# A fused transformer block on one core: zero matmuls in TensorE's waits, and a new order of the setup

## The chip, the cores and the metric

The kernel runs on one core of a Trainium2 chip. Its engines work side by side, each through its own list of instructions in order: TensorE (PE, matmuls; its weight loads are shown as PEld), VectorE (DVE), ScalarE (ACT), GpSimd (POOL) and SyncE (SP), which here only issues DMAs. Engines wait for one another by semaphores. The metric is device microseconds for one execution; several executions are run and their median is compared.

## The reference

One block of a diffusion transformer, for 16 samples (B) of 256 tokens (N) and width 256 (H), with 16 heads of 16, all in float32:

```
c_proj = silu(c) @ W_mod + b_mod                 # six vectors a sample
shift_a, scale_a, gate_a, shift_m, scale_m, gate_m = split(c_proj, 6)

x_norm = ln(x) * (1 + scale_a) + shift_a
q, k, v = split(x_norm @ W_qkv + b_qkv, 3)
x = x + gate_a * (softmax(q k^T / 4) v @ W_proj + b_proj)

q_c = ln(x) @ W_qc + b_qc
k_c, v_c = split(ln(context) @ W_kvc + b_kvc, 2)
x = x + softmax(q_c k_c^T / 4) v_c @ W_cproj + b_cproj

h = gelu((ln(x) * (1 + scale_m) + shift_m) @ W_mlp1 + b_mlp1)
out = x + gate_m * (h @ W_mlp2 + b_mlp2)
```

## The kernel before

**Units.** An attention of one sample is a unit: a self-attention ("s") or a cross-attention ("c"). There are 32, in the order s0, s1, s2, s3, then s4, c0, s5, c1 and so on; the last four are c12 to c15. After them comes the MLP of all samples in chunks.

**Precision.** Matmuls that must be exact run as three products of split operands (a high and a low part in float32r): `mm3` and `mm3_tok` issue six matmuls for one half of a projection. The high parts are made on ACT, the low parts on DVE or POOL. Matmuls of plain float32 (the zeros, the small columns of the setup, ps_ga, ps_pb) are written as two records each in the trace.

**A unit's work.** `layernorm` has three steps: statistics (DVE), reciprocal root (a power on POOL) and application. `transposed` turns the result on PE (tile psT), and makes its high part (xTh, ACT) and low part (xTl, DVE). `to_stack` projects to K or Q, makes h_k or h_q on ACT and l_k or l_q on DVE, and `send` copies their rows by DMA into a stack (tile big; three stacks are used in turn). A stack is zeroed once at the start, and row 63 of each half holds ones in K and the negative maxima in Q. `to_v` projects V into tile v, whose other columns are ones. Then come eight beats in which `s_tile` computes scores for the row maxima (tile s, PE) and one DVE reduction (tile mx) takes them; `m_part` transposes the maxima (psm), and two DMAs put them into the stack. In the eight beats after that, `t_part` computes the transposed scores (tile st, PE), ACT takes the exponential (tile pt), and `av_part` multiplies by V (tile o). Normalisation and projection out follow.

**The order of the work.** `beat(n, k)` writes beat k of unit n: the exponentials of unit n beside the maxima of unit n + 1, and pieces of the projections of units n + 2 and n + 3. There, projections run in lanes (`lane`, `lanes`): a lane contracts over half of the array's rows, and two lanes run side by side. `n` begins at -1, where only the maxima of unit 0 are made. All engines keep the written order.

**What stands ahead of the beats.** A string of words, `PRE`, gives the order of the setup; `SL` adds words to single beats. Here `L0a`, `L0b`, `L0d` are the layernorm steps of unit 0 (d: applied on DVE), `T0t`, `T0h`, `T0l` its transposes, high and low part, `K0a`, `K0b`, `K0l` the two halves of its projection K and the low part, `K0x0`, `K0y1p` and so on the sends of a half of the rows (with p: issued by POOL, else by SP), `z1kp` the zeroing of K's half of stack 1 on POOL, `ld2` the load of x of unit 2, `one0` the rows of ones of stack 0.

**The setup.** `setup_first` is a generator: each word `first` runs it to its next `yield`. It loads two parts of W_mod and three of W_qkv, then x of unit 1, takes silu of the condition, and has `busy(7)` and `busy(1)`, matmuls of zeros (wz, tile ps_warm). `cols_wide` makes scale and shift as rows (16 x 256), copies them on ACT and transposes them back to columns; `cols` makes the bias columns bk, bq, bv. `setup_rest` is a generator too: it loads all the remaining weights of the attention (wga, wp_f, wkc_f, wqc_f, wvc_f, wcp_f) and biases in its first step, then makes the gate (ps_ga, ps_pb, tile gb, stored to gd), and splits the weights one after another.

The projections of unit 0, and K of unit 1, stand ahead of the beats; Q and V of unit 1 and K of unit 2 run in lanes inside the eight beats n = -1. Issues of one engine are in order, so what stands behind a waiting instruction waits too; a DMA that SP issues waits on SP for its data.

Of the kernel before, what the change touches and what calls it, by code (L numbers as in the profile page):

```python
# [21 lines left out]
def pixart_block(  # L22
# [32 lines left out]
    E_ = {'M': ((-17, -12, -10, -1, 1), (0, 3, 4, 7, 9), (8, 11, 13, 15)), 'CUT': 8, 'LN': {'s': 'pool', 'c': 'pool', 'q': 'pool'}, 'ON': (1, 1, 1), 'L0': -16, 'L1': 1, 'S0': -7, 'A0': 0, 'T0': 1, 'H': (7, 11, 14, 15), 'S1': 5, 'A1': 7, 'L2': 9, 'T1': 9, 'S2': 32, 'AP': 23, 'DV': (0, 1), 'HP': (0, 0), 'BZ': {}, 'AV': {1: [(1, 2), (1, 3)], 9: [(0, 0), (0, 1)]}, 'AHEAD': (0, 0, 0, 0, 0, 2), 'W1P': [(-9, 1), (-8, 1), (-7, 1), (-6, 1), (-5, 1), (-5, 5), (-4, 1), (-4, 3), (-4, 5), (-3, 1), (-3, 3), (-3, 5), (-2, 1)], 'W2P': [(-4, 7), (-3, 0), (-3, 4), (-3, 6), (-3, 7), (-2, 2), (-2, 4), (-2, 6), (-1, 0), (-1, 1)], 'XP': 1, 'IL': 1, 'MF': 0, 'SH': 4, 'RAMP': 1, 'HA': 1, 'MP': 16, 'W': (7, 1, 0, 0), 'PRE': 'z0q first L0a L0b L0d z1kp z0k ld2 L1a first first T0t ld3 L1b z1qp first T0h T0l first one0 K0a z2kp z2qp rest K0b K0x0 L1d K0y0p first K0l K0l0 Q0a Q0b T1a Q0l Q0x0 Q0l0 Q0y0p Q0y1p T1b K0l1 Q0l1 K0y1p V0a K0x1p V0b K1a K1b Q0x1 ld4', 'SL': {(-1, 0): 'one1 one2', (-1, 2): 'first', (-1, 4): 'rest', (-1, 6): 'rest', (0, 0): 'rest', (0, 2): 'rest', (0, 4): 'rest', (0, 6): 'rest', (1, 3): 'rest'}}  # L55
# [49 lines left out]
    load_x(0)  # L105
    brow = const.tile([32, P], F32, name="brow")
    SP.dma_start(brow, bias_rows)
# [26 lines left out]

    def cols(dst, src, rhs, bias, name):

        pst = ps_gen(f"ps_{name}")
        n = 0
        for w in src:
            for t in range(w.shape[2] // P):  # L140
                for k in range(KC):
                    PE.matmul(pst[:, n * B:(n + 1) * B], w[:, k, t * P:(t + 1) * P], rhs[:, k],
                              start=(k == 0), stop=(k == KC - 1))
                n += 1
        DVE.tensor_tensor(dst, pst[:, :n * B].rearrange("p (n b) -> p n b", b=B),
                          bias.unsqueeze(2).to_broadcast([P, n, B]), ALU.add)
# [15 lines left out]
    def busy(n):  # L162
        if n == 0:
            return
        pst = ps_gen("ps_warm")
        for _ in range(n):
            PE.matmul(pst[:, :P], wz, wz, start=True, stop=True)

    def setup_first():

        ts = [work.tile([P, 2, KC, H], F32, tag="pt", name=f"wf{i}", bufs=5) for i in range(3)]
        wm = {c: stage(W_mod, c * H, "", t=ts[0][:, c]) for c in (1, 0)}
        wk, wq = [stage(W_qkv, c, "", t=ts[1][:, i]) for i, c in enumerate((H, 0))]
        load_x(1)
        wv = stage(W_qkv, 2 * H, "", t=ts[2][:, 0])
        dummy = const.tile([P, 2], F32, name="dummy")
        ACT.activation(dummy, mhalf, AF.Tanh)
        ACT.activation(th, c_sb, AF.Tanh, scale=0.5)
        DVE.scalar_tensor_tensor(th, th, 1.0, c_sb, ALU.add, ALU.mult)
        DVE.tensor_scalar(th, th, 0.5, None, ALU.mult)  # L180
        for v in vts:
            POOL.memset(v[:, :, :, HD:], 1.0)
        yield
        busy(E_['W'][0])
        pst = ps_gen("ps_silu")
        for k in range(KC):
            PE.transpose(pst[:, k * B:(k + 1) * B], th[:, k * P:(k + 1) * P], ident[:B, :B])
        ACT.copy(sT.rearrange("p k b -> p (k b)"), pst[:, :KC * B])
        pst = ps_gen("ps_brow")
        PE.transpose(pst[:, :32], brow, ident[:32, :32])  # L190
        ACT.copy(bT, pst[:, :32])
        busy(E_['W'][1])
        ACT.copy(Wk[0], wk)
        POOL.tensor_tensor(Wk[1], wk, Wk[0], ALU.subtract)
        scale = cols_wide(cpT[:, 2:4], wm[1], sT, bT[:, BMOD + 2:BMOD + 4], "scale")
        shift = cols_wide(cpT[:, 0:2], wm[0], sT, bT[:, BMOD:BMOD + 2], "shift")
        next(scale)
        ACT.copy(Wq[0], wq)
        POOL.tensor_tensor(Wq[1], wq, Wq[0], ALU.subtract)
        next(shift)  # L200
        busy(E_['W'][2])
        yield
        next(scale, None)
        DVE.tensor_scalar(sc1[:, 0], cpT[:, 2:4], 1.0, None, ALU.add)
        yield
        next(shift, None)
        busy(E_['W'][3])
        yield
        cols(bqkv[:, 2:4], [wk], cpT, bT[:, BQKV + 2:BQKV + 4], "bk")
        yield  # L210
        cols(bqkv[:, 0:2], [wq], cpT, bT[:, BQKV:BQKV + 2], "bq")
        ACT.copy(Wv[0], wv)
        DVE.tensor_tensor(Wv[1], wv, Wv[0], ALU.subtract)
        yield
        cols(bqkv[:, 4:6], [wv], cpT, bT[:, BQKV + 4:BQKV + 6], "bv")

    def setup_rest():
        gb = work.tile([B, 2, 2, H], F32, tag="pt", name="gb", bufs=5)
        gA, bb = gb[:, 0], gb[:, 1]
        bc = const.tile([1, H], F32, name="bc")  # L220
        wg, wp = stage(W_mod, 2 * H, "wga", "g", 3), stage(W_proj, 0, "wp_f", "g", 3)
        wkc, wqc = stage(W_kvc, 0, "wkc_f", "g", 3), stage(W_qc, 0, "wqc_f", "c", 2)
        wvc, wcp = stage(W_kvc, H, "wvc_f", "x1", 5), stage(W_cproj, 0, "wcp_f", "x1", 5)
        SP.dma_start(bb[:, 0], b_mod[2 * H:3 * H].partition_broadcast(B))
        SP.dma_start(bb[:, 1], b_proj.partition_broadcast(B))
        SP.dma_start(bc, b_cproj.partition_broadcast(1))
        yield
        pst = ps_gen("ps_ga")
        for k in range(KC):
            PE.matmul(pst[:B, :H], sT[:, k], wg[:, k], start=(k == 0), stop=(k == KC - 1))  # L230
        DVE.tensor_tensor(gA[:, 0], pst[:B, :H], bb[:, 0], ALU.add)
        yield
        pst = ps_gen("ps_pb")
        for k in range(KC):
            PE.matmul(pst[:B, :H], bqkv[:, 4 + k], wp[:, k], start=(k == 0), stop=(k == KC - 1))
        DVE.tensor_tensor(gA[:, 1], pst[:B, :H], bb[:, 1], ALU.add)
        DVE.tensor_tensor(gA[:, 1], gA[:, 1], gA[:, 0], ALU.mult)
        SP.dma_start(gd[:, 0:2], gA)
        yield
        split(Wp[0], Wp[1], wp)  # L240
        yield
        split(Wkc[0], Wkc[1], wkc)
        yield
        split(Wqc[0], Wqc[1], wqc)
        yield
        split(Wvc[0], Wvc[1], wvc)
        yield
        pst = ps_gen("ps_cb")
        for k in range(KC):
            PE.matmul(pst[:1, :H], bT[:, BKVC + 2 + k:BKVC + 3 + k], wcp[:, k],  # L250
                      start=(k == 0), stop=(k == KC - 1))
        DVE.tensor_tensor(bc, pst[:1, :H], bc, ALU.add)
        SP.dma_start(cd, bc)
        split(Wcp[0], Wcp[1], wcp)
# [139 lines left out]
    def to_stack(W, src, bias, dst, which, name):  # L394
# [8 lines left out]
        def first():  # L403
            o.ps = ps_gen(f"ps_{name}")
            mm3(o.ps[:, 0:N], W, 0, src.xT)

        def second():
            mm3(o.ps[:, N:], W, 1, src.xT)
            high()
# [30 lines left out]
        o.parts = [first, second, low]  # L440
        o.low_pool = low_pool
# [6 lines left out]
    def to_v(W, src, vt, name):  # L448
# [3 lines left out]
        def first():  # L452
            o.ps = ps_gen(f"psv_{name}")
# [122 lines left out]
    sp = psum.tile([P, 2, 512], F32, tag="s", name="s", bufs=1)  # L576
# [36 lines left out]

    st = psum.tile([P, 2, 512], F32, tag="st", name="st", bufs=1)
# [227 lines left out]
    w1, w2, first, rest = mlp_w1(), mlp_w2(), setup_first(), setup_rest()  # L842
# [8 lines left out]
    for n, v in (("0", u0), ("1", u1), ("2", u2)):  # L851
# [6 lines left out]
        word["L" + n + "d"] = lambda v=v: v.ln[0].steps[2]("dve")  # L858
        word["T" + n + "a"] = lambda v=v: (v.T[0].turn(), v.T[0].high())
        word["T" + n + "b"] = v.T[0].low  # L860
    for n, v in (("0", u0), ("1", u1), ("2", u2)):
        word["T" + n + "t"], word["T" + n + "h"], word["T" + n + "l"] = v.T[0].parts
        word["T" + n + "p"] = v.T[0].low_pool
        for c in "KQ":
            o = getattr(v, c)
            word[c + n + "l"] = o.parts[2]
            word[c + n + "p"] = o.low_pool
# [16 lines left out]
    for n in range(9):  # L884
        word[f"b{n}"] = lambda n=n: busy(n)
    for n in (2, 3, 4):
        word[f"ld{n}"] = lambda n=n: load(units[n])
    word["rest"] = lambda: next(rest, None)
    word["first"] = lambda: next(first, None)
# [32 lines left out]
    def beat(n, k):  # L922
        cur, prev, nxt = unit(n), unit(n - 1), unit(n + 1)
# [8 lines left out]
        soon = q3 if n < 0 else None  # L932
        q3T = q3 if not soon else None
# [5 lines left out]
        if k == 0 and q2:  # L939
            if n >= 0:  # L940
                q2.K.high()
# [27 lines left out]
        elif k == 1:  # L969
# [5 lines left out]
            if soon:  # L975
                soon.ln[0].steps[0]()
        elif k == 2:
# [8 lines left out]
            if soon:  # L986
                soon.ln[0].steps[1]()
                soon.ln[0].steps[2]()
# [9 lines left out]
        elif k == 4:  # L998
# [9 lines left out]
            if soon:  # L1008
                soon.T[0].turn()
                soon.T[0].high()  # L1010
                soon.T[0].low()
# [146 lines left out]
```

## Time and profile before

| | us |
|---|---|
| median of three runs | 828.48 (826.91 to 828.72) |
| the profiled execution, its time | 827.59 |
| its span, first to last instruction | 825.8 |
| PE busy | 782.7 |
| first matmul of s that waits (unit 0) | 28.57 |
| first matmul of s of unit 1, start of beat (0, 0) | 49.61 |
| first exponential (unit 0) | 50.90 |
| first exponential of unit 1 / of unit 2 | 68.87 / 87.96 |

A row of the timeline has the start and the duration in us, the engine, the line (L51 for all, the helper that records operations), the operation, the tile written and the tiles read, their shapes and the number of instructions merged; in brackets stands how long the engine had been idle before and what ended that. A row of the windows has the stretch, its length, the busy time and number of instructions of PE, PEld, DVE, ACT and POOL, the granted clock of TensorE (1.00 is full), the busy share of the DMA engines, and GB/s. A busy PE is not PE at its peak: at half the granted clock the same matmuls show as longer.

### The profile page before, as it was taken

What the parts mean: (1) busy time and instruction counts of PE and PEld (TensorE: products, weight loads), DVE (VectorE), ACT (ScalarE), POOL (GpSimd) and SP (SyncE); (2) the same over time, 40 slices, a digit from 0 to 9 for tenths busy, and PEclk for the clock granted to TensorE, in tenths of its full rate; (3) what the DMA queues carried; (4) which work ended last, traced back from release to release, by engine and by line L of the source; (5) the groups of instructions that cost most, each with busy time, mean ns of one, the idle gap of its engine ahead of it and who ended that gap; (6) DMA issues with size and microseconds to landing.
All of it is one profiled execution on the core that took longest, in us unless ns stands there. A gap on an engine that the chain in (4) does not pass through costs nothing.

```text
span 825.8 us, 23598 instructions
## 1 busy us (share of the span) xinstructions
PE 782.7 (95%) x9395; PEld 657.3 (80%) x9395; DVE 605.9 (73%) x1058; ACT 585.5 (71%) x1024; POOL 458.2 (55%) x398
## 2 busy tenths in 40 slices
PE   7789999999999999999999999999889999999997
PEld 6667777787787877777777787877558999999997
DVE  8488788888878788888788888777664566666562
ACT  3146888787887878888787888887556666666663
POOL 7125565663646546475563668655445666566663
PEclk9699999999999999999999999999899999999999
DMA  6434444343444535345344554434311222212211
GB/s 212 112 93 118 118 116 136 88 129 103 133 122 112 149 93 146 104 121 153 88 136 113 153 142 126 143 110 118 105 54 40 67 62 78 64 53 77 77 35 56
DMA packets 89841, 87.87 MB, mean 106 GB/s; under 512 B 9506, under 2 KB 85444, under 8 KB 89732
## 3 DMA queue, kind: packets, MB, share of 16 engines
q1 hardware_dynamic: 89492, 85.71, 36.9%
q8 instruction: 74, 1.21, 0.7%
q0 software_dynamic: 240, 0.66, 0.3%
q14 instruction: 35, 0.29, 0.1%
HBM read 26.97 MB, written 8.46 MB: 43 GB/s over the span
## 4 chain that ended last, share of the span: by engine, by line
PE 69%; DVE 19%; issue 5%; POOL 3%; DMA 2%; ACT 1%; SPq 0%; POOLq 0%; ACTq 0%
PE s L51 15%; PE o L51 12%; DVE mx L51 12%; PE ph L51 10%; PE st L51 9%; PE ps_q L51 4%; PE ps_kc L51 3%; PE ps_k L51 3%; PE ps_P_s L51 2%; PE ps_qc L51 2%; PE ps_v_s L51 2%; DVE xTl_s L51 1%; PE ps_P_c L51 1%; PE psm L51 1%; PE psT_m L51 1%
## 5 line engine op out<-in xcount | busy, mean ns | idle before, releaser
L51 DVE TENSOR_REDUCE mx<-s 128x4 f32<-128x1024 f32 x256 | 313.1, 1223 | 115.7 <-PE s L51 110.6
L51 ACT ACTIVATE pt<-st 128x1024 f32<-128x1024 f32 x256 | 260.9, 1019 | 47.2 <-PE st L51 40.3
L51 PE MATMUL s<-big 63*128 63x256 f32 x1024 | 125.1, 314 | 23.4 <-DVE mx L51 16.3
L51 PEld LDWEIGHTS s<-big 63*128 63x128 f32 x1024 | 82.9, 189 | 61.5 <-DVE mx L51 35.7
L51 PE MATMUL o<-pt,v 128*32 128x256 f32 x2048 | 125.5, 386 | 2.9 <-DVE A_s L51 2.9
L51 POOL TENSOR_TENSOR hl<-hf,hh 128x512 fp32r<-128x512 f32 x64 | 89.0, 1399 | 55.5 <-ACT hh L51 54.5
L51 PE MATMUL st<-big 64*128 64x256 f32 x1024 | 108.1, 283 | 2.0 <-ACT pt L51 2.0
L51 PEld LDWEIGHTS o<-pt,v 128*32 128x32 f32 x2048 | 60.8, 110 | 45.3 <-DVE A_s L51 5.2
L51 PEld LDWEIGHTS st<-big 64*128 64x128 f32 x1024 | 82.9, 189 | 3.8 <-ACT pt L51 2.9
L51 ACT COPY oT<-o 128x512 f32<-128x512 f32 x63 | 36.9, 586 | 47.6 <-PE o L51 47.6
L51 ACT ACTIVATE hf<-ph,bT 128x256 f32<-128x256 f32 x120 | 50.3, 473 | 28.1 <-PE ph L51 28.1
L51 ACT ACTIVATE hh<-ph,bT 128x256 fp32r<-128x256 f32 x120 | 50.4, 471 | 24.8 <-PE s L51 13.0
L51 POOL TENSOR_TENSOR xTl_as<-y_as,xTh_as 128x512 fp32r<-128x512 f32 x16 | 20.3, 1270 | 64.1 <-ACT y_as L51 64.1
L51 POOL TENSOR_TENSOR xTl_c<-y_c,xTh_c 128x512 fp32r<-128x512 f32 x16 | 20.6, 1290 | 62.0 <-PE s L51 52.9
L51 PE MATMUL ph<-wqch,wself 128*128 128x256 f32 x256 | 51.8, 285 | 0.0
L51 PE MATMUL ph<-wkch,wself 128*128 128x256 f32 x256 | 51.8, 286 | 0.0
L51 POOL TENSOR_TENSOR xTl_ac<-y_ac,xTh_ac 128x512 fp32r<-128x512 f32 x16 | 20.5, 1281 | 54.8 <-ACT y_ac L51 50.9
L51 PE MATMUL s<-big,hh 128*128 128x256 f32 x256 | 47.4, 282 | 0.0
L51 PE MATMUL st<-big,hh 128*128 128x256 f32 x256 | 47.2, 281 | 0.0
L51 DVE TENSOR_SCALAR xn_m<-x,mv_m,rs_m 128x256 f32<-128x256 f32 x32 | 38.2, 1234 | 10.8 <-POOL rs_m L51 10.8
L51 PEld LDWEIGHTS ph<-wqch,wself 128*128 128x128 f32 x256 | 42.0, 191 | 0.4 <-issue 0.4
L51 PEld LDWEIGHTS ph<-wkch,wself 128*128 128x128 f32 x256 | 41.9, 191 | 0.4
(234 smaller groups left out, 2373.3 us busy)
## 6 DMA issues: line engine op xcount, KB each, us to landing
big<-h_kc SPq DMA_DIRECT2D x64, 128.0 KB
big<-h_qc SPq DMA_DIRECT2D x64, 128.0 KB
big<-h_q SPq DMA_DIRECT2D x62, 128.0 KB
big<-h_k SPq DMA_DIRECT2D x61, 128.0 KB
x<-in_x_dram SPq DMA_DIRECT2D x16, 256.0 KB
big<-l_k SPq DMA_DIRECT2D x32, 128.0 KB
big<-l_q SPq DMA_DIRECT2D x32, 128.0 KB
c<-in_ctx_dram SPq DMA_DIRECT2D x16, 256.0 KB
```

Source lines behind the costliest of these rows:

```text
L51: i = f(*a, **k)
```

## The change

Three things are edited.

**Setup.** The generator `setup_first` becomes single words (`load`, `silu`, `turn`, `brow`, `scale`, `sc1`, `shift`, `bk`, `hik`, `lok` and so on). The loads stand in the order wm1 (scale), the bias rows, wk, wm0 (shift), wq, x of unit 1, wv; x of unit 0 is issued by ACT. Scale and shift are made as columns by `cols` at once, without `cols_wide`. The factor 0.5 of silu goes from DVE into ACT's copy. Both halves of stack 0 are zeroed on POOL at the start. `setup_rest` loads the remaining weights in three steps instead of one, and its steps move: the first to beat (-1, 6), ps_ga to (0, 1), ps_pb and the store gd to (0, 3), the last loads to (0, 4), the splits to (0, 5), (0, 6), (1, 1), (1, 3) and (1, 5).

**First two units.** K and Q of units 0 and 1 and V of unit 0 are projected whole, with all 128 rows of the array, ahead of the beats. V of unit 1 and K of unit 2 are projected whole inside the beats n = -1. `beat` does nothing but `visit` for n < 0; what it did there is in the words of `SL`.

**Zeros.** `busy` gets a place to write to. Ten, three times four, and five matmuls of zeros stand in the setup (words b10, b4, b5), 18 in the beats n = -1 (c4, c5, c4, c3, c2), seven in unit 0 (d4, d3), ten in units 30 and 31 (d3, d2, d3, d2). Before, there were eight.

```diff
-'PRE': 'z0q first L0a L0b L0d z1kp z0k ld2 L1a first first T0t ld3 L1b z1qp first T0h T0l first one0 K0a z2kp z2qp rest K0b K0x0 L1d K0y0p first K0l K0l0 Q0a Q0b T1a Q0l Q0x0 Q0l0 Q0y0p Q0y1p T1b K0l1 Q0l1 K0y1p V0a K0x1p V0b K1a K1b Q0x1 ld4'
-'SL': {(-1, 0): 'one1 one2', (-1, 2): 'first', (-1, 4): 'rest', (-1, 6): 'rest', (0, 0): 'rest', (0, 2): 'rest', (0, 4): 'rest', (0, 6): 'rest', (1, 3): 'rest'}
+'PRE': 'z0qp z0kp load silu b10 brow L0a turn L0b b4 L0d scale T0t sc1 hik lok T0h T0l b4 shift b4 hiq L1a L1b bk loq K0a K0b K0x0 K0x1 K0y0p K0y1p L1d T1t K0l T1h K0l0 K0l1 Q0a Q0m bq Q0h Q0x0 Q0y0p Q0x1 Q0y1p T1l Q0l Q0l0 Q0l1 z1kp z1qp K1a K1b hiv lov Q1a Q1b K1x0 K1x1 K1y0 K1y1 K1l K1l0 K1l1 ld2 Q1x0 Q1x1 Q1y0 Q1y1 Q1l Q1l0 Q1l1 V0a V0b bv b5 one0 vone ld3 z2kp z2qp'
+'SL': {(-1, 0): 'one1 one2 c4', (-1, 1): 'ld4 L2a V1a', (-1, 2): 'L2b L2c V1b', (-1, 3): 'c5', (-1,4): 'M0 c4', (-1, 5): 'T2t T2h T2l c3', (-1, 6): 'rest L3a K2a', (-1, 7): 'K2m L3b L3p L3c c2', (0, 0): 'rest d4', (0, 1): 'rest', (0, 2): 'd3', (0, 3): 'rest', (0, 4): 'rest', (0, 5): 'rest', (0, 6): 'rest', (1, 1): 'rest', (1, 3): 'rest', (1, 5): 'rest', (30, 0): 'd3', (30, 1): 'd2', (30, 2): 'd3', (31, 1): 'd2'}
...
     def cols(dst, src, rhs, bias, name):
-        pst = ps_gen(f"ps_{name}")
+        pst = st[:, len(spots) % 2, 2 * B * len(spots):]
+        spots.append(name)
...
-    def busy(n):
-        if n == 0:
-            return
-        pst = ps_gen("ps_warm")
+    def busy(n, where):
         for _ in range(n):
-            PE.matmul(pst[:, :P], wz, wz, start=True, stop=True)
+            PE.matmul(where[:, :P], wz, wz, start=True, stop=True)
...
-    def setup_first():
...
-        scale = cols_wide(cpT[:, 2:4], wm[1], sT, bT[:, BMOD + 2:BMOD + 4], "scale")
-        shift = cols_wide(cpT[:, 0:2], wm[0], sT, bT[:, BMOD:BMOD + 2], "shift")
...
+    def f_load():
+        X[0] = work.tile([P, NT, H], F32, tag="x", name="x_0", bufs=5)
+        ACT.dma_start(X[0], tok(x, 0))
+        stage(W_mod, H, "", t=wm1)
+        SP.dma_start(brow, bias_rows)
+        stage(W_qkv, H, "", t=wk)
+        stage(W_mod, 0, "", t=wm0)
+        stage(W_qkv, 0, "", t=wq)
+        load_x(1)
+        stage(W_qkv, 2 * H, "", t=wv)
...
+    def f_turn():
+        pst = st[:, 1, 480:]
+        for k in range(KC):
+            PE.transpose(pst[:, k * B:(k + 1) * B], th[:, k * P:(k + 1) * P], ident[:B, :B])
+        ACT.mul(sT.rearrange("p k b -> p (k b)"), pst[:, :KC * B], 0.5)
...
+    def f_scale():
+        cols(cpT[:, 2:4], [wm1], sT, bT[:, BMOD + 2:BMOD + 4], "scale")
+    def f_sc1():
+        DVE.tensor_scalar(sc1[:, 0], cpT[:, 2:4], 1.0, None, ALU.add)
+    def f_shift():
+        cols(cpT[:, 0:2], [wm0], sT, bT[:, BMOD:BMOD + 2], "shift")
...
     def setup_rest():
...
-        wkc, wqc = stage(W_kvc, 0, "wkc_f", "g", 3), stage(W_qc, 0, "wqc_f", "c", 2)
-        wvc, wcp = stage(W_kvc, H, "wvc_f", "x1", 5), stage(W_cproj, 0, "wcp_f", "x1", 5)
...
         SP.dma_start(bc, b_cproj.partition_broadcast(1))
+        yield
+        wkc, wqc = stage(W_kvc, 0, "wkc_f", "g", 3), stage(W_qc, 0, "wqc_f", "c", 2)
         yield
...
         SP.dma_start(gd[:, 0:2], gA)
+        yield
+        wvc, wcp = stage(W_kvc, H, "wvc_f", "x1", 5), stage(W_cproj, 0, "wcp_f", "x1", 5)
         yield
...
-        def second():
+        def third():
             mm3(o.ps[:, N:], W, 1, src.xT)
+
+        def second():
+            third()
             high()
...
+        word[f"b{n}"] = lambda n=n: busy(n, sp[:, 0])
+        word[f"d{n}"] = lambda n=n: busy(n, ps_gen("ps_warm", SHORT))
+        word[f"c{n}"] = lambda n=n: busy(n, st[:, 1])
...
     def beat(n, k):
+        if n < 0:
+            visit(n, k)
+            return
```

In the new order PE runs: ten zeros, the transposes of the bias rows and of silu, four zeros, scale, the transposes of unit 0, four zeros, shift, four zeros, bk, K of unit 0, the transposes of unit 1, Q of unit 0, bq, K and Q of unit 1, V of unit 0, bv, five zeros, and then the first s.

## The prediction

> **What bounds the kernel now.** I read the page first (shares of the engines, slices, chain), then the windows around its weak slices, then the timeline there.
>
> ```profile
> PE 782.7 (95%) x9395; PEld 657.3 (80%) x9395; DVE 605.9 (73%) x1058; ACT 585.5 (71%) x1024; POOL 458.2 (55%) x398
> PEclk9699999999999999999999999999899999999999
> ```
>
> PE is busy 95% of the span, so elsewhere than in the weak slices only less PE work would help, and the change takes none away. Weak in the clock row are the second and third slice (20 to 62 us) and the one at about 600 us. The windows name the stretches:
>
> ```profile
> core 0: us, PE busy (x) PEld busy (x) DVE busy (x) ACT busy (x) POOL busy (x), PEclk, DMA share, GB/s
> 16.20:26.40 10.20, 5.81 (x45) 5.30 (x44) 4.93 (x9) 3.85 (x9) 4.42 (x6) 1.00 0.96 251
> 26.40:40.20 13.80, 10.86 (x66) 9.85 (x67) 7.05 (x13) 0.57 (x2) 3.15 (x3) 0.51 0.26 67
> 40.20:53.90 13.70, 10.42 (x92) 7.57 (x92) 11.75 (x21) 4.86 (x10) 4.39 (x4) 1.00 0.37 100
> 53.90:57.20 3.30, 3.30 (x24) 2.75 (x26) 2.02 (x3) 1.85 (x4) 1.05 (x2) 0.50 0.31 84
> 593.20:600.00 6.80, 5.91 (x50) 2.98 (x48) 4.45 (x11) 2.19 (x3) 4.48 (x4) 0.50 0.13 43
> ```
>
> Three stretches at half the clock, 23.9 us in all; the first follows a stretch in which PE idled 4.4 us while the DMA engines were 96% busy. There the timeline shows the stage of the maxima of unit 0 (tile s, reduced on DVE):
>
> ```profile
> 28.57 0.77 PE L51 MATMUL s<-big 63*128 63x256 f32 x3 [1.11 <-DMA big<-h_q]
> 29.38 1.22 DVE L51 TENSOR_REDUCE mx<-s 128x4 f32<-128x1024 f32 x1 [7.41 <-PE s L51]
> 45.88 0.50 PE L51 MATMUL s<-big 63*128 63x256 f32 x4 [0.75 <-DVE mx L51]
> 47.71 0.50 PE L51 MATMUL s<-big 63*128 63x256 f32 x4 [0.36 <-DVE mx L51]
> 49.61 0.57 PE L51 MATMUL s<-big 63*128 63x256 f32 x4
> ```
>
> The first s waits for the last rows of Q of unit 0; eight beats go from 28.57 to 49.61, 21.0 us, though the last two take 1.83 and 1.90 us, the pace of s, the 1.22 us reduction and two hand-overs.
>
> **The change, part by part.** *Setup, until the first s.* Rows used:
>
> ```profile
> 1.05 3.36 PE L51 MATMUL ps_warm<-wz 128*128 128x128 f32 x14 [1.05 <-DVE wz L51]
> 6.78 1.87 PE L51 MATMUL ps_scale<-wf,sT 128*16 128x256 f32 x4 [1.19 <-DMA wf<-in_L_xcond_W_mod_dram]
> 11.44 0.84 ACT L51 ACTIVATE xTh_s<-psT_s,sc 128x256 fp32r<-128x256 f32 x2 [1.06 <-DVE sc L51]
> 11.84 1.06 PE L51 MATMUL ps_bk<-cpT,wf 128*128 128x16 f32 x8 [0.83 <-DVE cpT L51]
> 13.20 4.79 DVE L51 TENSOR_SCALAR xn_s<-x,mv_s,rs_s 128x256 f32<-128x256 f32 x2
> 15.60 0.84 ACT L51 ACTIVATE h_k<-ps_k,bqkv 128x256 fp32r<-128x256 f32 x2 [3.33 <-PE ps_k L51]
> ```
>
> A zero matmul is two records, 3.36 / 7 = 0.48 us. At full clock I take 0.24, as the bias columns' eight records take 1.06 us at 1.00 (ps_bk) and 1.89 at 0.50 (ps_bv at 34.36).
> PE: ten zeros from 1.05 end at 5.85, the transposes of silu and bias rows at 6.3, four zeros at 7.3 (8.2 at half clock), the scale columns, eight records like ps_bk, at 8.3. W_mod's scale half landed at 6.75; it now leaves SP at 1.21 instead of 2.16, so it is there. The load of x of unit 0, now issued by ACT, puts 0.41 ahead of ACT's table load, hidden behind the ten zeros. Two small DVE steps (0.17, 0.32) give the scale at 8.8; the transposes of x (0.66) end at 8.95, since POOL's two memsets (1.8 each, from 1.3) and its power (0.71) end at 5.7 and the two normalisations then run without a memset beside them: 0.40 us each is the shortest row of this operation, 1.38 its usual one beside POOL. So xTh begins at 9.0 instead of 11.44. Then in PE's order four zeros, shift (1.06), four zeros, bk (1.06), to 12.9 (xTl, 0.88, ends at 10.8 inside that), K of unit 0 (12 x 0.12, the start-to-start of ps_q at 17 us) to 14.3: h_k at 14.35 instead of 15.60.
> Unit 1's normalisation is behind bk's add on DVE: 13.2, one of two beside POOL's weight split, 1.38 + 0.40, to 15.0 (before: 18.0, beside three memsets). Behind it queue unit 1's transposes (0.66), Q of unit 0 (1.44) and bq (1.06): 18.2. PE then waits for unit 1's xTl (add 0.2, 0.88) until 19.4; K and Q of unit 1, 2.8, to 22.2; V of unit 0 waits for the split of Wv, which sits behind h_k of unit 1 on ACT (0.62 + 0.68), to 23.2; 1.44, bv 1.06 and five zeros 1.2: first s at 26.9. The rows of Q do not end later: h_q 19.35, l_q 20.3, sends at 0.55 to 0.65 each on SP until 21.6; POOL's two sends landed 3.9 to 5.5 us after issue before, which makes 23 to 26. The six weight loads (1.5 MB, issued 11.84 to 14.83) that kept the DMA engines at 0.96 are gone from here. First s 1.7 us earlier (half clock all through the setup: 31.9, 3.3 later; V and unit 1's work packed closer: 25).
> *Maxima.* Before, Q and V of unit 1 and K of unit 2 went through this stage in lanes of half the array, 48 matmul steps of time (only Q beside V and V beside K share a step); now V and K go whole, 24 steps, half a projection a beat (6 x 0.12 = 0.72). PE's fillings are, by beat: 0.96 zeros, 0.72, 0.72, 1.2 zeros, 0.28 + 0.96, 0.66 + 0.72, 0.72, 0.72 + 0.48. With s (0.45) each is at most 1.85, inside the beat of 1.85 that the reduction sets; DVE's statistics and xTl of unit 2 go over the 0.6 us gap between reductions by 0.13 twice and 0.28. 8 x 1.85 + 0.5 = 15.3: unit 0 begins at 42.2 instead of 49.61, **-7.4**. These zeros cost nothing only while the clock is full; at half clock four of them take 1.92 and the beat is theirs. SP's queue here holds unit 1's twelve sends, the loads of x2, x3 and x4 and six rows of ones, some 23 issues of 0.6 from 22.3 to 36.5; the row of maxima behind them is wanted at 42. POOL's memsets for v and for unit 2's stacks (3 x 0.48, 2 x 1.8) stand behind V's copy of unit 0 at 24.7 and ahead of unit 2's power and normalisation (3.1): 33 to 34, wanted by PE in the sixth beat at 36.
> *Unit 0.* The weight loads, ps_ga and ps_pb move in here. s began at 49.61, 51.50, 53.75, 55.90, 58.49. First beat: 0.96 zeros in an idle 0.86, +0.1. Second and fourth: PE had no wait, so ps_ga and ps_pb (1.04 each, 0.9 start to start) add: s and st 0.7, twelve steps 1.5, 0.9: 3.1 each instead of 2.25 and 2.59 (the latter at half clock). Third: 0.7 + 0.66 + 0.72 = 2.1 against 2.15. Together +1.4. On SP the store gd now stands ahead of h_q of unit 2, and gb is ready some 0.5 after h_q could leave; behind it wait the rows of l_q, whose landing at 67.61 released unit 2's s: +0.5. wkc and wqc fill an SP idle from 55.96 to 59.24. **+1.9**; bounds 0 (full clock alone saves this much) and +4 (four loads of 0.5 us on SP's chain besides).
> *Units 1 on:* two casts (0.42) and splits (1.28) move from unit 0 to unit 1; DVE was busy 14.16 of 18.20 there, so nothing, bounds 0 and 0.8.
> *Tail.* Cold beats:
>
> ```profile
> 574.29 0.50 PE L51 MATMUL s<-big 63*128 63x256 f32 x4 [0.50 <-DVE mx L51]
> 579.53 0.50 PE L51 MATMUL s<-big 63*128 63x256 f32 x4
> 589.30 0.51 PE L51 MATMUL s<-big 63*128 63x256 f32 x4
> 592.96 0.66 PE L51 MATMUL s<-big 63*128 63x256 f32 x4 [0.50 <-DVE mx L51]
> 596.40 3.64 PE L51 MATMUL o<-pt,v 128*32 128x256 f32 x32
> 600.56 0.51 PE L51 MATMUL s<-big 63*128 63x256 f32 x4
> ```
>
> The same two beats take 5.24 us a unit before and 7.60 here: 2.36 lost. The ten zeros: three before 589.30, where PE had no wait (+0.72); two in a wait of 0.86 (0); three in 0.50 (+0.2); two in 0.21 (+0.3). Net **-1.1** if the clock holds, +1.2 if not.
> The Trainium skill ("TensorE: Matmul & The Clock Gate", section "Why this matters for your kernels") has it that a gap of PE over some 3 us drops the clock; by it these ten zeros, and the seven of unit 0, would only cost. The rows say otherwise: in the 3.4 us before 593.2 and before 53.9 no PE wait was over 0.9 us and the clock still fell to 0.50, so a thin load is enough. By the page the tail would be +1.2, the whole 2.3 us worse.
>
> Sum: -7.4 + 1.9 - 1.1 = -6.6 on this execution's 827.59 us (span 825.8 and 1.8 around it): 821.0. The median shown, 828.48, lies 0.9 higher, so 821.9; I say **821.8**.
>
> **Rivals.** *The zeros do not hold the clock.* For it: seven zeros from 1.05 and one at 4.79 filled most of 1.05 to 5.6, yet scale at 6.78 still ran at 0.42 us per record, half clock. Against it: 26.40 to 40.20 stayed at 0.51 with PE 79% busy, but with matmuls of 63 and 64 rows; the zeros use 128. Price, with only the setup warm by its real matmuls: the maxima's fillings (8.1 in all) double to 16.3, with 8 x 0.65 of s at half clock (0.62 at 39.33, 0.80 at 30.65) 21.5 (+0.5 instead of -5.7), first s still -1.7, unit 0 +1.9 and 1.7 for zeros, tail +1.2 and 1.0: 828.48 + 4.6, **833**. It decides from a mean beat of 2.7 us in the maxima (6.6 / 8 over 1.85).
> *SP's queue becomes the bound* in the maxima and unit 0, x2 or the stacks of unit 1 landing late: for it the 7.41 us wait above and the l_q chain; against it 1.5 MB less at that time. Half of the maxima's gain lost (2.9) and +3 instead of +1.9: -2.6, **826**.
> *The setup packs better:* first s at 25, unit 0 at +0.4 instead of +1.9: -10.0, **818.5**.
>
> **How the numbers follow.** Forecast 0.57 (its own range 818.5 to 825), zeros 0.18, SP queue 0.14, better packing 0.11. What differs by under 0.2% (1.7 us) can't be told from no change. Slower: the zeros' case and a little of SP's, 0.20; same: 0.05, from SP's; faster 0.75. The range leaves out the upper part of the zeros' case and the lowest packing: 816.5 to 830.
>
> **What would show it.** Granted clock 1.00 from about 8 us to the end of unit 0 and at 585 to 600 us; first s near 27, first exponential near 43.5 (50.90 before); mx every 1.85 us; ps_ga and ps_pb inside unit 0. Wrong: a clock of 0.5 in the maxima, or s waiting there for big<-h_q, or units 0 and 1 together, first exponential to first exponential of unit 2, over 41 us (50.90 to 87.96, 37.1, before; 39 forecast).

## The result, and the profile after

The changed kernel takes 820.0 us (median of 14 executions, 818.99 to 826.1), the kernel before 828.47 (14, 826.74 to 830.46): a ratio of 0.9907, 95% interval 0.989 to 0.9924 (the ratios here lie near those of the means; the medians alone give 0.9898). The forecast was 821.8, in a range of 816.5 to 830.

Two executions of the 14 lie at 824.6 and 826.1, the others at 819.0 to 821.9. The first profile happens to be of the 824.57 one (span 822.8); a second profile, from the run called after_again below, is of one of 820.06 (span 818.3). Both are needed. From the page of the first, the two lines that answer to those shown of before:

```profile
PE 789.5 (96%) x9471; PEld 667.1 (81%) x9471; DVE 598.1 (73%) x1055; ACT 585.1 (71%) x1022; POOL 462.2 (56%) x399
PEclk9999999999999999999999999999999999999999
```

No slice of the clock row is weak any more; for the first slice that says nothing, as is shown below. The windows of the second profile, cut at the same stages (columns as before: busy time and count of each engine, then the granted clock, the DMA share and GB/s):

```profile
16.20:25.20 9.00, 8.17 (x64) 7.47 (x62) 4.30 (x11) 3.62 (x8) 6.98 (x8) 1.00 0.78 219
25.20:40.20 15.00, 13.03 (x98) 10.31 (x97) 12.13 (x19) 2.00 (x5) 5.68 (x5) 1.00 0.55 162
40.20:53.90 13.70, 13.52 (x141) 9.81 (x140) 10.36 (x19) 7.37 (x13) 3.14 (x3) 1.00 0.38 111
53.90:59.70 5.80, 4.97 (x60) 4.49 (x61) 4.91 (x11) 4.35 (x6) 5.07 (x5) 1.00 0.57 158
585.00:592.60 7.60, 6.29 (x75) 4.35 (x75) 6.39 (x15) 4.23 (x6) 3.21 (x3) 1.00 0.12 37
```

Second row: the maxima of unit 0, 15.0 us at 1.00 where there were 21.0 us, mostly at 0.50. Last row: the tail's beats at 1.00, where 593.2 to 600.0 had 0.50. Its timeline shows the beats, one s a beat:

```profile
25.23 0.51 PE L51 MATMUL s<-big 63*128 63x256 f32 x4
27.05 0.50 PE L51 MATMUL s<-big 63*128 63x256 f32 x4 [0.23 <-DVE mx L51]
28.88 0.50 PE L51 MATMUL s<-big 63*128 63x256 f32 x4 [0.41 <-DVE mx L51]
...
40.22 0.68 PE L51 MATMUL s<-big 63*128 63x256 f32 x4
```

Every s of these eight beats takes 0.50 or 0.51, and the next comes 1.82 to 1.83 us after it, but for one beat of 2.24; the s at 40.22 already belongs to unit 0. What still ends the waits is the reduction on DVE (mx).

The two profiles part in the setup. Timeline of PE, first of the 820.06 execution, then of the 824.57 one (wz are the zeros, st<-sT the scale columns, s<-big the first s):

```profile
1.05 4.55 PE L51 MATMUL s<-wz 128*128 128x128 f32 x20 [1.05 <-DVE wz L51]
6.04 1.16 PE L51 MATMUL s<-wz 128*128 128x128 f32 x8 [0.17 <-ACT bT L51]
7.04 0.96 PE L51 MATMUL st<-sT,wf 128*128 128x16 f32 x8
```

```profile
1.05 4.64 PE L51 MATMUL s<-wz 128*128 128x128 f32 x20 [1.05 <-DVE wz L51]
6.20 2.08 PE L51 MATMUL s<-wz 128*128 128x128 f32 x8
8.07 1.73 PE L51 MATMUL st<-sT,wf 128*128 128x16 f32 x8
...
30.90 0.50 PE L51 MATMUL s<-big 63*128 63x256 f32 x4
```

The same instructions, 1.16 against 2.08 and 0.96 against 1.73. In the one the clock rose just as the ten zeros ended, in the other not before 20.2 us, in K of unit 0; the first s stands at 25.23 and 30.90, and of these 5.7 us 5.6 are still there at unit 4 and 4.5 at the end. The clock row of the page has 9s there all the same: it shows full clock until the first change is recorded, so in a setup the durations must be read, not the clock row.

Where the time went is read from five marks of each profile: the first s (where a wait parts its four matmuls, the row behind the wait), the copy m at the start of unit 0, of the fifth unit (called unit 4) and of unit 30 on ACT, and the end of the span. All later runs are in the table too; the last column is the median of all executions of the run.

| kernel | first s | unit 0 | unit 4 | unit 30 | end | median |
|---|---|---|---|---|---|---|
| before | 28.57 | 50.72 | 123.63 | 587.60 | 825.8 | 828.5 |
| after (824.57) | 30.90 | 47.12 | 121.92 | 585.45 | 822.8 | 820.0 |
| after_again | 25.23 | 41.43 | 116.29 | 581.08 | 818.3 | 820.6 |
| no_setup_zeros | 25.08 | 42.06 | 119.69 | 582.84 | 820.0 | 821.9 |
| no_maxima_zeros | 25.04 | 42.90 | 118.55 | 582.01 | 819.2 | 825.9 |
| no_tail_zeros | 31.14 | 47.36 | 121.98 | 586.61 | 823.9 | 821.2 |
| order_alone | 26.53 | 45.89 | 124.58 | 588.25 | 826.6 | 827.4 |
| zeros_alone | 29.75 | 55.05 | 126.77 | 591.17 | 828.5 | 829.7 |
| long_setup_zeros | 26.38 | 42.59 | 118.22 | 581.63 | 818.9 | 821.1 |
| rest_early | 24.74 | 41.02 | 112.53 | 576.91 | 814.1 | 816.5 |
| gb_own | 24.74 | 40.96 | 116.21 | 579.77 | 816.9 | 823.6 |
| early_no_b4 | 27.29 | 43.60 | 115.13 | 579.77 | 817.0 | 819.4 |
| early_no_setup | 26.19 | 43.27 | 114.88 | 578.41 | 815.5 | 816.5 |
| early_no_zeros | 25.89 | 43.84 | 117.49 | 582.11 | 820.2 | 821.9 |

From unit 4 to unit 30 all fourteen profiles need 463.2 to 464.8 us: no edit acts there, and a difference of two profiles below 1.6 us can be chance of that stretch. By stage, after_again against before: first s -3.3, maxima (first s to m of unit 0) 16.20 against 22.15, -6.0; unit 0 to unit 4 74.86 against 72.91, +1.95; the middle +0.8; from unit 30 to the end 237.22 against 238.20, -1.0. Together -7.5, as the spans have it.

### The profile page after: what moved, and what is told of

It reads as the page before. It is cut to its first block, busy times and chain, and to the rows that moved or that the text cites. A ratio compares the mean times of both kernels' runs of the same rounds, so it can differ in the third digit from the quotient of the medians.

```text
span 822.8 us, 23741 instructions
## 1 busy us (share of the span) xinstructions
PE 789.5 (96%) x9471; PEld 667.1 (81%) x9471; DVE 598.1 (73%) x1055; ACT 585.1 (71%) x1022; POOL 462.2 (56%) x399
## 4 chain that ended last, share of the span: by engine, by line
PE 68%; DVE 18%; issue 4%; POOL 3%; DMA 1%; ACT 1%; SPq 0%; POOLq 0%; ACTq 0%
PE s L51 15%; PE o L51 13%; DVE mx L51 13%; PE ph L51 10%; PE st L51 9%; PE ps_q L51 3%; PE ps_kc L51 3%; PE ps_k L51 2%; PE ps_qc L51 2%; PE ps_P_s L51 2%; DVE xTl_s L51 1%; PE ps_v_s L51 1%; PE ps_P_c L51 1%; PE psm L51 1%; PE psT_m L51 1%
## 5 line engine op out<-in xcount | busy, mean ns | idle before, releaser
L51 PE MATMUL s<-big 63*128 63x256 f32 x1024 | 121.0, 309 | 16.9 <-DVE mx L51 13.7
L51 PE MATMUL o<-pt,v 128*32 128x256 f32 x2048 | 123.8, 382 | 3.1 <-DVE A_s L51 3.1
L51 PEld LDWEIGHTS s<-big 63*128 63x128 f32 x1024 | 80.1, 185 | 54.0 <-DVE mx L51 33.2
L51 POOL TENSOR_TENSOR xTl_as<-y_as,xTh_as 128x512 fp32r<-128x512 f32 x16 | 20.4, 1272 | 63.0 <-ACT y_as L51 63.0
```

Source lines behind the costliest of these rows:

```text
L51: i = f(*a, **k)
```

## The experiments

The theory: the gain comes from a clock that no longer falls in the setup, the maxima and the tail, for which order and zeros are both needed, and unit 0 pays for the columns moved into it. The rivals: the order alone is the gain and the zeros stand in the way; or the zeros alone are.

**The change again, and without one group of its zeros each** (four runs on one chip; before there 827.84).

> The changed kernel once more, as the partner of the other three of this call and to see a second trace of it: its profiled execution took 824.57 us, 4.6 above its median of 820.0. In that trace the zeros of the setup ran at 0.23 us a record and scale, shift and bk at 1.73 each, half clock, until 20.2 us; the first s began at 30.9 instead of the forecast 26.9. If the clock in the setup is what parts the executions, a trace of one near 820 has scale or bk near 1.0 us and the first s near 26 to 28. If it is something else, the first s is at 31 there too and the 4.6 us lie later. Times: about 820, some 824 to 826.

820.6 (819.56 to 825.9, six executions, two of them at 825.6 and 825.9); ratio 0.9926, 0.9896 to 0.9955. The second profile is from here.

```
-silu b10 brow ... L0b b4 L0d ... T0l b4 shift b4 hiq ... bv b5 one0
+silu brow ... L0b L0d ... T0l shift hiq ... bv one0
```

> The 27 zeros of the setup (10, 4, 4, 4, 5) left out, nothing else. Theory A (the zeros of the setup lift the clock in the executions near 820): without them scale, shift, bk and K of unit 0 are at half clock, and the time is 1 to 3 us over the changed kernel. Theory B (zeros do not lift the clock, and at half clock they stand in PE's way: 10.53 to 12.2 and 13.8 to 15.65 in the trace): bk ends near 13 instead of 17.4, the first s near 26 to 27 instead of 30.9, and the time is 2 to 4.5 us under the profiled 824.6, so 0 to 1 us under 820 or a little less.

821.87 (821.58 to 823.31); ratio 0.9928, 0.9909 to 0.9947: 1.3 more than the change, as theory A had it, and no execution apart. But its whole early setup is at half clock (scale columns 1.89, bias columns of K 1.89), and yet the first s comes at 25.08, and the second at 27.34 against 27.05 in the good execution of the change (after_again): here theory B was right. So without zeros in PE's queue the half clock leaves this setup only some 0.3 us behind; the twelve zeros between the columns cost 2.08 + 1.91 + 2.05 us when the clock has not risen. Most of its loss is later, in unit 0, where the fifth exponential (timeline of ACT and PE) comes late:

```profile
55.52 1.02 ACT L51 ACTIVATE pt<-st 128x1024 f32<-128x1024 f32 x1 [3.12 <-DMA gd<-gb]
56.59 0.50 PE L51 MATMUL st<-big 64*128 64x256 f32 x4 [2.25 <-ACT pt L51]
```

An exponential that waits for the landing of a store of biases: gb lies in one of the five buffers of the ring pt, and the buffer is needed for the fifth exponential. PE waited 2.25 us, the clock was 0.71 in the 5 us around it, and unit 0 took 22.6 us (42.06 to 64.62) instead of 19.4. The same wait stands in the change, shorter (PE then waits 0.51 us for st):

```profile
53.15 1.02 ACT L51 ACTIVATE pt<-st 128x1024 f32<-128x1024 f32 x1 [1.38 <-DMA gd<-gb]
```

The store is issued at 52.10 here and ends the wait 3.4 us later, in after_again 1.7 us after 51.47. Whether leaving out the zeros made it slower, one profile does not show.

```
-'one1 one2 c4' ... (-1, 3): 'c5' ... 'M0 c4' ... 'T2t T2h T2l c3' ... 'K2m L3b L3p L3c c2'
+'one1 one2' ... 'M0' ... 'T2t T2h T2l' ... 'K2m L3b L3p L3c'
```

> The 18 zeros in the eight beats of the maxima left out, nothing else. Theory A (they hold the clock): it falls to 0.5 in the maxima, beats grow from 1.83 to some 2.0 to 2.3 and unit 0 begins at half clock: 2 to 4 us slower. Theory B (the whole-array projections ahead of the stage and in four of its beats hold it): beats stay at 1.83, the time stays within 0.5 us.

825.9 (821.03 to 831.75, twelve executions); ratio 0.9988, 0.9964 to 1.0012. Theory A, and more than it said: without these eighteen zeros the gain is gone in the median. The profile is of the fastest execution, and even there the clock falls in the sixth beat:

```profile
32.34 0.50 PE L51 MATMUL s<-big 63*128 63x256 f32 x4 [1.32 <-DVE mx L51]
34.16 0.80 PE L51 MATMUL s<-big 63*128 63x256 f32 x4 [1.11 <-DVE mx L51]
36.28 0.80 PE L51 MATMUL s<-big 63*128 63x256 f32 x4 [0.27 <-DVE mx L51]
38.97 0.80 PE L51 MATMUL s<-big 63*128 63x256 f32 x4
```

Beats of 1.82 us become 2.1 to 2.7. No wait of PE in these beats is over 1.32 us. This execution is 2.3 us behind after_again at unit 4; what the eleven slower ones lose beyond that no profile shows.

```
-(30, 0): 'd3', (30, 1): 'd2', (30, 2): 'd3', (31, 1): 'd2'
```

> The ten zeros of units 30 and 31 left out, nothing else. Theory A (they hold the clock): the granted clock falls to 0.5 near 590 us for 3.4 to 6.8 us again, the two beats from the third s of unit 30 take 7.6 instead of 5.2, and the kernel is 1.0 to 2.4 us slower. Theory B (the clock falls or not by where its windows lie, the zeros only add): same or up to 1.2 us faster.

821.24 (818.83 to 825.67); ratio 0.9919, 0.9891 to 0.9946: not to be told from the change. The clock does fall once, as the product o shows (1.93 us at full clock):

```profile
593.80 0.56 PE L51 MATMUL s<-big 63*128 63x256 f32 x4 [1.09 <-DVE mx L51]
595.03 3.14 PE L51 MATMUL o<-pt,v 128*32 128x256 f32 x32
```

Unit 30 takes 20.11 us here against 19.54 with the zeros, and the rest 217.18 against 217.68: the zeros give 0.6 and take 0.5. Against before the tail is 0.9 better all the same, since the clock here was down for 3.4 us and not 6.8.

**Order alone, zeros alone, and the setup's clock** (one chip, before there 827.53).

> The change without any of its zeros: the new order of setup and loads and the whole projections alone. Theory A (order and zeros need each other: with nothing in PE's waits the clock falls in the maxima, as it did in most executions without the zeros there, and the setup is cold): the first s near 25, as without the setup's zeros, then beats of 2.2 us and more, unit 0 begins after 42.5; 825 to 828.5, so that of the 8 us no more than 3 come from the order alone. Theory B (the order is the gain and the zeros are only a help): unit 0 begins before 41.5, 821 to 823.5.

The zeros of all three groups above are out (27, 18 and 10), and the seven of unit 0. 827.43 (822.98 to 829.41, twelve executions); ratio 0.9987, 0.9968 to 1.0007. Theory A: the new order by itself gains nothing that can be told. Windows of its profile:

```profile
26.00:36.00 10.00, 7.19 (x33) 5.27 (x33) 6.19 (x11) 0.59 (x1) 6.30 (x6) 0.59 0.65 184
36.00:45.00 9.00, 7.64 (x35) 5.74 (x36) 6.53 (x11) 1.69 (x5) 0.98 (x2) 0.50 0.31 95
45.00:55.00 10.00, 9.42 (x47) 6.51 (x45) 4.87 (x6) 3.92 (x7) 2.62 (x3) 0.50 0.47 134
55.00:57.00 2.00, 2.00 (x31) 1.77 (x30) 1.76 (x3) 1.46 (x3) 0.00 (x0) 0.99 0.00 0
```

The clock falls at the start of the maxima, at 27.7, and rises only at 55.0, though PE is busy for 9.42 of the last 10 us before that. By the table: the maxima 3.2 us longer than in after_again (19.36 against 16.20), units 0 to 3 3.8 longer, the tail 1.1, the first s 1.3.

The reverse, on the kernel before (the zeros of the maxima, of unit 0 and of the tail; its setup keeps its own eight):

```
-'SL': {(-1, 0): 'one1 one2', (-1, 2): 'first', (-1, 4): 'rest', (-1, 6): 'rest', (0, 0): 'rest', (0, 2): 'rest', ... (1, 3): 'rest'}
+'SL': {(-1, 0): 'one1 one2 b4', (-1, 2): 'first', (-1, 3): 'b5', (-1, 4): 'rest b4', (-1, 5): 'b3', (-1, 6): 'rest', (-1, 7): 'b2', (0, 0): 'rest b4', (0, 2): 'rest b3', ... (1, 3): 'rest', (30, 0): 'b3', (30, 1): 'b2', (30, 2): 'b3', (31, 1): 'b2'}
-        pst = ps_gen("ps_warm")
+        pst = ps_gen("ps_warm", SHORT)
```

> The kernel before, in its own order, with the change's zeros in the beats of the maxima, in unit 0 and in the tail. Theory A (the clock fell there only because PE waited): the clock holds, the eight beats of the maxima take 16 to 18 us instead of 21.0 and unit 0 begins by 47; 823 to 826. Theory B (what stands in those beats, projections in lanes of half the array, does not hold the clock, and zeros beside it are work in the way): the s still take 0.77 us in the middle of the maxima; 827.5 to 831.

829.71 (828.71 to 833.65, twelve executions); ratio 1.0026, 1.0012 to 1.004. Theory B: slower by 2.2. The s, after the first of them:

```profile
32.44 0.79 PE L51 MATMUL s<-big 63*128 63x256 f32 x4
...
37.97 0.80 PE L51 MATMUL s<-big 63*128 63x256 f32 x4
42.83 0.50 PE L51 MATMUL s<-big 63*128 63x256 f32 x4
```

The zeros do raise the clock, but late, between the s at 37.97 and the one at 42.83, and until then they cost twice their time in beats that the half-array lanes already fill: first s to m of unit 0 25.30 us against 22.15. They repay part of it: units 0 to 3 -1.2, the tail -0.9 (238.2 to 237.33). So the order alone gives 0, the zeros alone lose 2, and both together gain 7 to 8: in the new order the beats have room in which the zeros fit, and the zeros keep the clock at which the shorter beats are worth something. That it is the whole projections that make this room, rather than another part of the new order, is argued; no run takes them alone.

```
-silu b10 brow
+silu b16 brow
```

> The changed kernel with sixteen zeros instead of ten at the start of the setup (7.4 us at half clock instead of 4.6). Theory A (zeros lift the clock only if they fill one whole stretch of some 3.4 us of a count that runs freely, so that 4.6 us of them are enough in some executions and not in others): all executions set up at full clock, scale columns 0.96 each in the profile, the first s at 25.5 to 27; no execution of the undisturbed ones over 823, the median 820 to 821.5. Theory B (the two kinds of setup have another cause, such as the chip's state before the launch): executions at 824 to 826 stay about one in five, the others are 0.5 to 2 slower, median 821 to 823.

821.14 (820.34 to 824.9); ratio 0.9928, 0.9905 to 0.9952. The profile has the setup of theory A (scale columns 0.96, first s 26.38), but two of six executions are at 824.6 and 824.9: more zeros do not do away with them, as A said they would.

One thing in the traces goes with an early or a late rise. In each profile all recorded changes of the clock lie whole multiples of 3.413 us apart, and where this grid stands against the start differs from execution to execution. In after_again the ten zeros fill its stretch from 1.96 to 5.38 wholly, and the clock rises at 5.38; in the 824.57 execution they fill the stretch from 3.16 to 6.58 to 85%, and it does not rise. Nine profiles have seven or ten zeros at the start: in five zeros fill a stretch to 87 to 100%, and the clock rises at its end (also in zeros_alone); in four (after, no_tail_zeros, early_no_b4, before) they fill none to more than 85%, and it rises later, in three of them not before 17.4 us. That agrees with theory A and is no proof of it: sixteen zeros fill a whole stretch wherever the grid stands, and of the two late executions of this run there is no profile.

**Loads of the remaining weights early.** In the change the DMA engines stand idle from 10 to 16 us, and the two columns of setup_rest with their store gd go into unit 0.

```
-z0qp z0kp load silu b10 ...
+z0qp z0kp load rest silu b10 ...
-(-1, 0): 'one1 one2 c4' ... (-1, 3): 'c5' ... (-1, 6): 'rest L3a K2a'
+(-1, 0): 'one1 one2 rest' ... (-1, 3): 'rest' ... (-1, 6): 'L3a K2a'
-(0, 0): 'rest d4', (0, 1): 'rest', (0, 2): 'd3', (0, 3): 'rest', (0, 4): 'rest', (0, 5): 'rest'
+(0, 0): 'd4', (0, 2): 'd3', (0, 5): 'rest'
         SP.dma_start(bc, b_cproj.partition_broadcast(1))
-        yield
         wkc, wqc = ...
+        wvc, wcp = ...
         yield
...
         SP.dma_start(gd[:, 0:2], gA)
         yield
-        wvc, wcp = ...
-        yield
```

> The changed kernel with the loads of the remaining weights (seven tiles and three bias rows) right behind the first loads, where the DMA queues stand idle from 10 to 16 us, and the gate and projection-bias columns with their store gd in beats 0 and 3 of the maxima, in the place of the nine zeros there. Theory A (what unit 0 lost, +1.4, and the wait of its fifth exponential for the store gd, 1.4, come back): no wait on gd<-gb in unit 0, h_q of unit 2 leaves at its product, unit 0 takes 17.9 to 18.3 from first m to the next unit's; 818 to 819.5. Theory B (the early loads stand ahead of the rows of K and Q of unit 0 on the queues, or the columns' adds on DVE lengthen the beats of the maxima): first s over 26 or unit 0 beginning after 41; 820 to 823.

816.5 (815.87 to 821.74, one of six above 817.2); ratio 0.9873, 0.9847 to 0.99: faster than theory A said, by 4.1 than the change. Two stretches of its timeline:

```profile
24.74 0.50 PE L51 MATMUL s<-big 63*128 63x256 f32 x4
25.17 1.04 PE L51 MATMUL ps_ga<-wga,sT 128*16 128x256 f32 x4
26.56 0.50 PE L51 MATMUL s<-big 63*128 63x256 f32 x4 [0.35 <-DVE mx L51]
...
48.57 2.62 SPq L51 DMA_DIRECT2D big<-h_q  x4
```

ps_ga and ps_pb (1.04 each) stand in waits that zeros had filled, and the beats stay at 1.82. h_q of unit 2 leaves 7.5 us after m of unit 0; in the change it was these lines of SP, 10.5 us after it, behind the store:

```profile
51.47 0.34 SPq L51 DMA_DIRECT2D gd<-gb  x1
51.94 2.52 SPq L51 DMA_DIRECT2D big<-h_q  x4
```

Unit 0 takes 16.45 us (41.02 to 57.47) against 19.40, and units 0 to 3 71.51 against 74.86.

The run moves loads, columns and store together, so it does not part what each is worth.

**What of that is the wait on gd, and what the zeros still do** (one chip, before there 827.56).

```
-        gb = work.tile([B, 2, 2, H], F32, tag="pt", name="gb", bufs=5)
-        gA, bb = gb[:, 0], gb[:, 1]
+        gA, bb = [work.tile([B, 2, H], F32, tag="x1", name=n, bufs=5) for n in ("gA", "bb")]
```

> The changed kernel, only that the gate and bias columns (gb) lie in two buffers of the ring x1 instead of one of the five buffers of the ring pt, so that the fifth exponential of unit 0 no longer has to wait until the store gd<-gb has landed. Loads, columns and their places in unit 0 are as in the changed kernel. Theory A (that wait, 1.38 us on ACT, is on the path): no wait on gd<-gb, 1.0 to 1.6 faster than the changed kernel's 820 to 821. Theory B (PE waits only 0.51 us for that exponential; the loss of unit 0 is the columns' time on PE and the rows of h_q behind them): 0.3 to 0.6 faster, 819.8 to 820.5.

823.57 (818.7 to 829.09, twelve executions, spread over the whole of it); ratio 0.9958, 0.993 to 0.9985. In the times neither theory. In the profile, of the fastest execution, the wait is gone, and unit 0 takes 19.03 us instead of 19.40, the 0.3 to 0.6 of theory B, but unit 1 20.37 instead of 19.60: from unit 0 to unit 4 75.25 against 74.86, nothing gained. Unit 1 need not be the edit's doing, for it takes 20.4 us in long_setup_zeros too, with gb in its old place. So this wait, 1.38 us long on ACT, is 0.4 us of what unit 0 lost; what is left are the columns, the loads and h_q behind the store, which no run parts. Why eight of the twelve executions took 821.6 to 829.1 no profile shows. Their granted clock is 0.995 to 1.000, that of the four fast ones 0.997 to 1.000, so a clock that fell later on, as in no_maxima_zeros, explains little of it; a late rise in the setup would not show in that figure, but was worth 5.7 us where it was seen, and the slowest are 10 us over the fastest.

```
-L0b b4 L0d ... T0l b4 shift b4 hiq
+L0b L0d ... T0l shift hiq
```

> rest_early without the three groups of four zeros around the scale, shift and bias columns of the setup; the ten at the start and the five at the end stay. Theory A (the executions 4 to 6 us above the others are those whose setup ran at half clock, and there the twelve zeros, 1.9 to 2.1 us a group, stand in the way of the first s): no execution 4 us above the lowest, all within 2.5 us, median 815.5 to 817. Theory B (the late executions have another cause): one in six to one in three still 4 to 6 us above the others, median 816 to 817.5.

819.39 (817.84 to 822.03); ratio 0.9896, 0.9879 to 0.9912, slower than rest_early and still spread over 4 us: both theories missed. Its profile has the clock low until K of unit 0 (scale columns 1.89); the ten zeros that are left end at 5.69 and hold the scale columns back from 5.90 to 6.40, and the five at the end cost 1.36: first s 27.29. So in this profile ten zeros that don't raise the clock are worse than none (early_no_setup, next).

```
-silu b10 brow ... L0b b4 L0d ... T0l b4 shift b4 hiq ... bv b5 one0
+silu brow ... L0b L0d ... T0l shift hiq ... bv one0
```

> rest_early without any zeros in the setup (27 matmuls), those of the maxima, of unit 0 and of the tail as in rest_early. Theory A (the setup is bound by loads and by small steps, at whichever clock, and once the store gd is out of unit 0 nothing is left that a late clock costs): first s 25 to 25.6, unit 0 16.4 to 17.5, no execution 4 us above the others; 816 to 817.5. Theory B (the zeros of the setup are worth what they were in the changed kernel, 1.3 us, or more, since the clock falls in a later stage): 817.5 to 820.

816.52 (816.04 to 817.32, four executions); ratio 0.9861, 0.9847 to 0.9875. Theory A in the median and the spread; the first s, at 26.19, is 0.6 later than it said:

```profile
5.90 1.89 PE L51 MATMUL st<-sT,wf 128*128 128x16 f32 x8 [0.29 <-ACT sT L51]
...
26.19 0.81 PE L51 MATMUL s<-big 63*128 63x256 f32 x4
26.93 1.04 PE L51 MATMUL ps_ga<-wga,sT 128*16 128x256 f32 x4
28.32 0.50 PE L51 MATMUL s<-big 63*128 63x256 f32 x4 [0.35 <-DVE mx L51]
```

It is the version to keep: as fast as rest_early with 27 fewer matmuls, and its four executions lie within 1.3 us.

The last takes out c4, c3, c2, d4, d3 and the four groups of the tail as well:

> rest_early without any zeros at all: the order and the early columns alone. Theory A (order and zeros need each other, as in the run of the order alone: real work in two of the eight beats of the maxima doesn't hold the clock): the s of the maxima at 0.80 each, unit 0 begins after 42.5; 820.5 to 825, the gain over the order alone (827.4) being what the early loads are worth, 3 to 4 us. Theory B (the columns in the beats of the maxima do the work of the zeros): clock 1.00 in the maxima, 816 to 818.5.

821.9 (819.7 to 826.0); ratio 0.9927, 0.9907 to 0.9948, and each theory is right for half of the maxima. The clock holds through the first six beats, two of which have ps_ga and ps_pb, and falls in the seventh:

```profile
35.86 0.51 PE L51 MATMUL s<-big 63*128 63x256 f32 x4 [1.18 <-DVE mx L51]
37.69 0.72 PE L51 MATMUL s<-big 63*128 63x256 f32 x4 [0.73 <-DVE mx L51]
39.92 0.80 PE L51 MATMUL s<-big 63*128 63x256 f32 x4
```

The 26 zeros of the later stages are worth 5.4 us (821.9 against 816.5), the early loads and columns 5.5 (827.43 to 821.9).

## Why the prediction was right

*Maxima:* 15.3 us forecast for the eight beats, 15.0 measured; the beat is 1.82 to 1.83 instead of 1.85 but for one of 2.24. That the zeros must hold the clock there was the first rival's question: no_maxima_zeros and order_alone show what comes without them, and that in this order they hold it. The rival (833) fell.

*Unit 0:* +1.9 forecast, 19.40 + 19.60 against 17.97 + 19.09 us measured for units 0 and 1, +1.9. The beats came as reckoned too: in after_again the s of the first four beats stand at 40.22, 42.22, 45.47, 47.40 and the next at 50.47, 10.25 us against 8.88 before, where the forecast had +1.4. From the first exponential of unit 0 to that of unit 2 it is 39.0 us (41.60 to 80.61), the 39 forecast. The cause named, two columns in beats without a wait and the store gd ahead of h_q, is what rest_early removes, and it removed more than was put there: units 0 to 3 become 1.4 us shorter than before the change (71.51 against 72.91). That extra is most likely the clock, which no longer falls at 53.9 us: zeros_alone, in the old order, has 71.72. The wait of the fifth exponential was not foreseen: gb's place in the ring pt was overlooked. It cost the change 0.4 us of unit 0 by gb_own, and 2.25 us of PE in no_setup_zeros. The second rival (826 by SP's queue) fell: units 0 and 1 lost what was reckoned and no more.

*Tail:* -1.1 forecast; from unit 30 to the end 237.22 us against 238.20, -1.0. In ten profiles with these zeros that stretch is 237.09 to 237.35, in the three kernels with no zeros after the setup 238.09 to 238.35. Yet no_tail_zeros needs 237.29, for in its profile the clock fell for 3.4 us and not for 6.8. The size was right for this execution of before; what the zeros are worth differs with how long the clock would have been down.

*Setup:* the term that was mis-sized. First s at 26.9 forecast, -1.7; 25.23 in the good execution, -3.3, which is 1.6 of the 1.8 us between 821.8 and the median of 820.0. The forecast priced each of the five groups of columns at 1.06 us, the length of its row; in after_again the next instruction starts 0.81 to 0.82 us after each, which makes 1.2 us of these 1.6. And the sum over PE's zeros and columns is not the only thing that sets the first s: no_setup_zeros, at half clock but without the zeros, has it at 25.08. The two bounds given, 25 and 31.9, lie beside two kinds of execution, 25.2 and 30.9. The upper one was reckoned for just this, half clock all through the setup; that the lower one fits is luck, for it was reckoned from a closer packing and not from the clock. The third rival (better packing, 818.5) was right in this half, a first s at 25, and wrong in the other, unit 0 at +0.4.

*A reading of the clock row:* the row of before has a 9 in its third slice, so it is not weak there as was read; the fall at 53.9 us is seen in the windows alone.

*The rule weighed:* by the section "Why this matters for your kernels" of the Trainium skill's page "TensorE: Matmul & The Clock Gate" a gap of over some 3 us drops the clock. Here it fell in no_maxima_zeros with no wait over 1.32 us, and stayed at 0.50 in order_alone while PE was busy 9.42 of 10 us. The measurement decides: such a gap is not needed, a thin load is enough, and the zeros of the maxima did what the forecast took from the rows.

## What to carry to other kernels

Shortening the work in a beat and keeping the clock may be worth nothing apart and 7 us together, so test the two halves of such a change alone before one is given the credit. In the place of zeros put real work that is due later anyway, its loads issued while the queues are idle: the early loads with two columns moved into the beats of the maxima gave 4 us more than the zeros there. Zeros belong where PE waits for another engine; ahead of work that is ready they cost their own time, at half clock about twice (2.08 us against 1.16 for four).

## What the runs showed of the hardware

- Whether the setup's zeros raise the clock differs between executions of one program: it rose while ten of them ran or just behind them (20 records in 3.90 us in rest_early and 4.55 in after_again, 4.64 at half clock), or, in the 824.57 execution, not before 20.2 us. The recorded changes lie whole multiples of 3.413 us apart, and in the profiles with zeros at the start the early rises are those where zeros filled a stretch of this grid to 87% or more. Every run with zeros between the columns of the setup had executions 4 us and more above its lowest. The two without any zeros in the setup, but with those of the maxima, unit 0 and the tail, had none in ten (no_setup_zeros 821.58 to 823.31, early_no_setup 816.04 to 817.32).
- PE's busy time does not tell whether the clock rises. In the 824.57 execution PE is busy for all of the 14.00 us from 6.2 to 20.2, with zeros, columns of 16 and transposes, and the clock stays low (the durations show it); it rises behind K of unit 0, on all 128 rows. In order_alone it stays at 0.50 from 45 to 55 us, with PE busy for 9.42 of 10, with s and st of 63 and 64 rows, lanes of half the array, and columns of 16. That the shape of the matmuls decides fits this, but no run changes the shape alone.
- A profile's granted clock reads 1.00 before the first recorded change, over matmuls that take twice their time (the eight records of the scale columns 1.73 instead of 0.96).
